# Row LSTM on one core: the odd pixels' output stays in PSUM for sum, difference and residual, the even residual moves to GpSimd, and the steady order is written anew

## The chip, the core and the metric

The kernel runs on one core of a Trainium2 chip. The engines are TensorE (PE in the profile; its weight loads are PEld), VectorE (DVE), ScalarE (ACT), GpSimd (POOL) and SyncE (SP, which here only issues DMAs). The metric is the device time of one execution in microseconds (us), as the median of several runs.

## The reference

The input x is 8 images of 96 channels, 128 x 128 pixels, in fp32. It is group-normalised, passed through a row LSTM and added to itself. The row LSTM goes down the rows of the image: each row's state depends on the row above, so the 128 rows cannot be computed at the same time.

```python
its = conv(X, W_is * mask, kernel 1x3) + b_is          # input part of the 4*96 gates
def step(carry, row_in):
    h, c = carry
    gates = conv(h, W_ss, kernel 3) + b_ss + row_in    # along the row
    f, i, o = sigmoid(...), sigmoid(...), sigmoid(...)
    g = tanh(...)
    c_new = f * c + i * g
    h_new = o * tanh(c_new)
    return (h_new, c_new), h_new
...
x = x + row_lstm(group_norm(x))
```

## The kernel before

**Half-steps.** The 8 images are split into two halves of 4, and the two run as two recurrences side by side. A half-step `n` is one row of one half; half-steps of the two halves alternate, and half 0 is one row ahead. So the result of half-step `n` is needed by half-step `n + 2`, and while it is being made the other half's products keep TensorE busy. There are 256 half-steps from 0 to 255 and one before; nearly all (2 to 253) run through one repeated order of work.

**Products.** Even and odd pixels of a row are kept apart, so that a product has 256 columns: 4 images by 64 pixel pairs. A half-step has three banks of gates, A, B and C, each one PSUM bank of 128 partitions by 512 columns, the left half for one and the right half for another partial product. The state enters the products in four forms: the sum of even and odd pixels ("vs", line 670), their difference ("vf", L674), and two shifted differences ("ve" in the tile te, L680, and "vo", L684). Products 1 and 2 take the sum and the difference; products 0 and 3 the shifted ones. P, Q and E are the products of the input rows ("xs"). Each product of one bank is two pieces, one for each row group of 64 partitions of the PE array, and the two row groups run at the same time. All are issued at line 512. After P, Q, 1 and 2, ScalarE copies the left half to SBUF (L583), VectorE adds the right half to it for the even pixels (L587) and subtracts it for the odd pixels (L591), and then 0, 3 and E are added on top.

**Gates.** ScalarE takes tanh (L596) and sigmoid (L615, and L618 for the last third of the output gate). VectorE multiplies the forget gate with the old cell state (L623); input gate times tanh is made by GpSimd for the even pixels (L630) and by VectorE for the odd ones (L632); then follow the new cell state (L642), its tanh on ScalarE into PSUM (L650) and the output h = o * tanh (L658), which is written into the tile hx. hx holds 128 partitions: 96 of the state, and 32 of normalised input channels which GpSimd (L337) and in part ScalarE (L335) write ahead. From hx come the sum, the difference and the shifted differences, and the residual (L700, VectorE, all 512 columns) adds h to the row of x that is stored.

**Input rows.** GpSimd also normalises the input (L337 into xw) and forms its sums and differences (L354, L358 into xs), one image and four rows at a time; this is the list of pieces that `work(n)` hands out, with the DMAs that go with them. `finish(n)` issues what is left of that list and the store of a finished block of four rows.

**Order.** The order on each engine is written by hand. The string PERIOD is one half-step's list, and each engine runs its own entries strictly in that order. An entry is a part's name and a bank; `a` and `b` at its end mean even and odd pixels; `'` means the half-step before, `+` the next one; for S, F, D0 and D1 (sum, difference, shifted even, shifted odd) two half-steps are added. `<` and `>` choose the row group. X and U are the pieces of `work` for hx on ScalarE and GpSimd; W1, W2, W3 are the three steps of the input rows. LAST is the list of the end. Names: cp copy, lo even (L587), hi odd (L591), ta tanh, si sigmoid, o2 the last third of the output gate, fg forget, gt gated, ce cell, th cell tanh, ou output, re residual.

**PSUM.** All gate banks come from one pool of 8 banks, three for a half-step, and are handed out in turn: a bank is written anew when everything that uses its earlier tile is through.

Of the kernel before, what the change touches and what calls it, by code (L numbers as in the profile page):

```python
# [8 lines left out]
AF = mybir.ActivationFunctionType  # L9
# [12 lines left out]
def kernel(  # L22
# [119 lines left out]
    hx = pair([P, R, 2, BH, JP], "hx")  # L142
# [274 lines left out]
    HB = BH * J  # L417
# [53 lines left out]
                self.waited = number  # L471

    lanes = Lanes()
    whole = slice(0, P)

    class HalfStep:


        def __init__(self, n):
            self.n, (self.row, self.s) = n, place(n)  # L480
            i, r = self.row // R % 2, self.row % R
            self.ps, self.m1, self.done, self.gates, self.outputs = {}, {}, set(), None, None
            self.moving = {"ve": te[self.s][:, i, r : r + 1]}
            self.started, self.images, self.halves, self.writer = set(), {}, {}, {}
            self.even_input = None
            self.hx, self.xs = hx[self.s][i][:, r], xs[self.s][i][:, r]
            self.c = cs[self.s].rearrange("p t b j -> p (t b j)")
# [164 lines left out]
        def output(self, lo=0, hi=BH, t=None):  # L652
            s, row = self.s, self.row
            nxt = hx[s][(row + 1) // R % 2][0:C, (row + 1) % R]
            self.h = strided(nxt[:, 0, 0, :], 0, [(BH * JP + 1, 2), (JP, BH), (1, J)])
            for t in range(2) if t is None else (t,):
                o, th = (self.part(ap, lo, hi, t) for ap in (self.o, self.tanh_of(t)))
                nc.vector.tensor_mul(self.h[:, t, lo:hi], o, th)  # L658

        def operand(self, name, parts=1):  # L660
            if name not in self.moving:
# [1 line left out]
            return self.moving[name].rearrange("p t (b j) -> p t b j", b=BH)  # L663

        def pair(self, lo, hi):
            return self.hx[:, 0, lo:hi, 0:J], self.hx[:, 1, lo:hi, 1 : J + 1]

        def total(self, engine=nc.vector, lo=0, hi=BH):
            e, o = self.pair(lo, hi)
# [20 lines left out]
        def residual(self, lo=0, hi=BH, t=None):  # L690
            s, row = self.s, self.row
            if t is not None:
                xo = xt[s, row // R][0:C, :, row % R, :].rearrange("p b (j t) -> p t b j", t=2)
                nc.vector.tensor_add(xo[:, t], xo[:, t], self.h[:, t])
                return
            xo = xt[s, row // R][0:C, :, row % R, :].rearrange("p b (j t) -> p t b j", t=2)
            if self.n < 1:
                nc.gpsimd.tensor_add(xo, xo, self.h)
            else:
                nc.vector.tensor_add(xo, xo, self.h)  # L700
# [31 lines left out]
    FIRST = [  # L732
        ([], own(0, 1, 1), own(0, 1, 2)),
        (shared(0, 1, 0), own(0, 1, 3), [(spare, 0, 1), (load_rows, 0, 2)]),
        (beside(0, 1, 1) + shared(0, 1, 2), own(1, 1, 0), []),
        (beside(0, 1, 3) + shared(1, 1, 0), own(1, 1, 1), []),
        (beside(1, 1, 1) + shared(1, 1, 2), own(1, 1, 2), []),
        (shared(1, 1, 3), own(1, 1, 3), [(spare, 1, 1), (load_rows, 1, 2), (load, 0, 2)]),
        (shared(0, 2, *SHARED[0]), own(0, 2, 0), []),
# [43 lines left out]
    def finish(n):  # L783
# [19 lines left out]
    LAST = (  # L803
        "2B'' 1A'' 1B'' 2A'' cpB'' 2C'' cpA'' loB'' hiB'' loA'' hiA'' 1C'' 0B'' EB'' 3A'' 0A'' "
        "3B'' cpC'' EA'' o2'' loC'' taA'' siA'' hiC'' 3C'' siBa'' 0C'' PA QA PB QB PC QC EA EB "
        "siBb'' fg'' taCb'' gtb'' taCa'' siC'' gta'' ceb'' thb'' cea'' oub'' tha'' oua'' F'' S'' "
        "D1'' D0'' re'' 1A 2A 1B 1C 2B 2C cpA loA hiA cpB loB 3A hiB 0A 0B 3B cpC loC hiC 0C 3C "
        "taA siA fg o2 siBa siBb taCa taCb gta gtb siC ceb cea thb tha oub oua reb rea"
    )
# [9 lines left out]
    }  # L819
    steps = {}  # L820

    def half_step(n):
        if n not in steps:
# [3 lines left out]
    def do(n, names, by_lanes=False):  # L827

        for name in names.split():
# [440 lines left out]
```

## Time and profile before

| | before |
|---|---|
| median of 3 runs | 2055.06 us (2054.9 to 2056.24) |
| the profiled execution | 2054.18 us, span 2052.4 us |
| granted TensorE clock | 0.995 |
| matmuls | 16400, one weight load each |
| DMA | 242.84 MB, mean 118 GB/s |

How to read the rows in the next sections. A row of totals gives the busy time of an engine, its share of the span and its instructions. A row of the stage table begins with the stretch (from:to in us from the span's start) and its length, then busy time and (xcount) for PE, PEld, DVE, ACT and POOL, then the granted clock, the DMA share and GB/s; for one line alone it has that line's engine only. A row of a timeline has the start in us, the duration in us (of all together where the count is over one), engine, line, operation, output and inputs, shape and count; in brackets the idle time before it and what ended it. A row of a group has line, engine, operation, tiles, shapes and count, then busy time in us and the mean in ns of one, then the idle time before it. A row of one source line gives the least, median and greatest duration in ns, and when it first and last ran.

### The profile page before, as it was taken

The page shows a single profiled execution, that of the slowest core. Times are in us where ns is not written, and L with a number is a line of the kernel's source. Part 1 is how long each engine was busy: PE and PEld are TensorE (multiplying, and loading weights), DVE is VectorE, ACT ScalarE, POOL GpSimd, SP SyncE. Part 2 cuts the span into 40 slices and gives each one's busy share as a digit, 9 for nine tenths or more (in the row PEclk, how much of TensorE's full clock was granted, in tenths as well). Part 3 has the DMA queues.
Part 4 walks back from the last instruction along what each step waited for, and adds up shares of the span by engine and source line. Part 5 has one row for each costly group of instructions (what it writes and reads, how often), then busy time and mean ns, then how long its engine had stood idle before and what let it go on. Part 6 is the DMA issues. An engine that isn't in the chain of part 4 may idle for free.

```text
span 2052.4 us, 46059 instructions
## 1 busy us (share of the span) xinstructions
PE 1980.4 (96%) x16400; PEld 1824.5 (89%) x16400; DVE 1904.3 (93%) x4018; ACT 1580.1 (77%) x3519; POOL 1568.0 (76%) x1917
## 2 busy tenths in 40 slices
PE   3679999999999999999999999999999999999998
PEld 0358999999999999999999999999999999999996
DVE  5788999999999999999999999999999999999997
ACT  6687777777777777777777777777777777777776
POOL 4358888888888888888888888888888888888851
PEclk9989999999999999999999999999999999999999
DMA  9983433444343344434334433433443343344311
GB/s 402 417 265 84 117 83 99 119 106 105 87 119 90 90 119 112 103 88 114 96 84 119 116 99 94 108 96 84 118 119 96 98 104 99 88 111 119 96 37 32
DMA packets 110290, 242.84 MB, mean 118 GB/s; under 512 B 6832, under 2 KB 16368, under 8 KB 104048
## 3 DMA queue, kind: packets, MB, share of 16 engines
q1 hardware_dynamic: 110064, 239.89, 43.0%
q8 instruction: 134, 2.20, 0.5%
q14 instruction: 92, 0.75, 0.1%
HBM read 181.34 MB, written 50.33 MB: 113 GB/s over the span
## 4 chain that ended last, share of the span: by engine, by line
PE 91%; DVE 3%; DMA 3%; ACT 2%; POOL 1%; issue 0%; SPq 0%; DVEq 0%; ACTq 0%; POOLq 0%
PE ps L512 90%; DMA xs<-in_x_dram 2%; DVE bst L1142 1%; DMA te<-in_x_dram 1%; DVE vf L674 0%; DVE ps L587 0%; ACT g L596 0%; DVE hx L658 0%; DVE vs L670 0%; POOL xw L337 0%; DVE ps L591 0%; DVE c L642 0%; ACT ps L615 0%; ACT ps L650 0%; PE rows L212 0%
## 5 line engine op out<-in xcount | busy, mean ns | idle before, releaser
L512 PE MATMUL ps<-vf,wm 64*128 64x256 f32 (+1 forms) x3046 | 847.2, 385 | 1.0 <-DVE vf L674 1.0
L512 PE MATMUL ps<-te,wl 64*128 64x256 f32 (+1 forms) x3042 | 790.1, 385 | 0.1
L512 PE MATMUL ps<-vo,wl 64*128 64x256 f32 (+1 forms) x3042 | 783.6, 382 | 2.2 <-DVE ps L591 2.1
L512 PE MATMUL ps<-vs,wm 64*128 64x256 f32 (+1 forms) x3046 | 748.0, 386 | 8.2 <-POOL vs L670 6.7
L512 PE MATMUL ps<-xs,wx 64*128 64x256 f32 (+1 forms) x3080 | 635.7, 377 | 2.0 <-POOL xs L354 1.8
L512 PEld LDWEIGHTS ps<-vf,wm 64*128 64x128 f32 (+1 forms) x3046 | 517.5, 186 | 22.6 <-DVE vf L674 2.9
L512 PEld LDWEIGHTS ps<-vs,wm 64*128 64x128 f32 (+1 forms) x3046 | 466.7, 186 | 41.7 <-POOL vs L670 9.5
L512 PEld LDWEIGHTS ps<-xs,wx 64*128 64x128 f32 x3080 | 490.9, 187 | 7.5 <-POOL xs L354 3.4
L512 PEld LDWEIGHTS ps<-vo,wl 64*128 64x128 f32 (+1 forms) x3042 | 458.2, 186 | 42.5 <-DVE ps L591 3.8
L512 PEld LDWEIGHTS ps<-te,wl 64*128 64x128 f32 (+1 forms) x3042 | 472.0, 186 | 20.9 <-PE ps L512 0.5
L583 ACT ACTIVATE m<-ps,wl 128x256 f32<-128x256 f32 x766 | 359.4, 469 | 95.1 <-PE ps L512 78.0
L630 POOL TENSOR_TENSOR g<-i,g 96x256 f32<-96x256 f32 x251 | 182.4, 727 | 307.8 <-ACT g L596 307.6
L587 DVE TENSOR_TENSOR ps<-m,ps 128x256 f32<-128x256 f32 x768 | 326.0, 425 | 17.8 <-ACT m L583 13.1
L591 DVE TENSOR_TENSOR ps<-m,ps 128x256 f32<-128x256 f32 x768 | 325.5, 424 | 17.5
L618 ACT ACTIVATE o<-ps 32x512 f32<-32x512 f32 x256 | 151.2, 591 | 224.2 <-PE ps L512 223.7
L596 ACT ACTIVATE g<-ps 32x512 f32<-32x512 f32 x765 | 313.6, 442 | 7.3 <-PE ps L512 0.6
L337 POOL TENSOR_SCALAR xw<-xr,rstd,nmr 128x512 f32<-128x512 f32 (+1 forms) x267 | 283.6, 1063 | 35.7 <-DVE nmr L329 11.5
L700 DVE TENSOR_TENSOR x<-x,hx 96x512 f32<-96x512 f32 x253 | 301.6, 1192 | 0.0
L512 PE MATMUL ps<-xs,wt 64*128 64x256 f32 x1012 | 299.2, 376 | 1.4 <-DVE ps L591 1.4
L358 POOL TENSOR_TENSOR xs<-xw 128x512 f32<-128x512 f32 (+1 forms) x254 | 293.0, 1154 | 0.0
L658 DVE TENSOR_TENSOR hx<-o,ps 96x256 f32<-96x256 f32 x512 | 213.4, 417 | 54.2 <-PE ps L512 30.5
L684 POOL TENSOR_TENSOR vo<-hx 128x256 f32<-128x256 f32 x257 | 258.7, 1006 | 5.7 <-PE ps L512 4.7
(118 smaller groups left out, 2569.3 us busy)
## 6 DMA issues: line engine op xcount, KB each, us to landing
xr<-in_x_dram SPq DMA_DIRECT2D x124, 512.0 KB, 6.4
x<-in_x_dram SPq DMA_DIRECT2D x62, 768.0 KB, 6.0
out_dram<-x SPq DMA_DIRECT2D x62, 768.0 KB, 4.8
xs<-in_x_dram SPq DMA_DIRECT2D x31, 1024.0 KB, 11.0
x<-in_x_dram SPq DMA_DIRECT2D x62, 256.0 KB, 3.1
te<-in_x_dram SPq DMA_DIRECT2D x8, 1024.0 KB, 11.2
hx<-in_x_dram SPq DMA_DIRECT2D x8, 1024.0 KB, 9.7
te<-xs SPq DMA_DIRECT2D x62, 128.0 KB, 3.2
```

The lines of the kernel that those rows point to most:

```text
L337: return engine.tensor_scalar(dst, src, scale, shift, ALU.mult, ALU.add)
L358: return engine.tensor_sub(differences, strided(xw[:, 0, :], 0, [(W + 1, n), (J + 1, 2), (1, J)]), strided(xw[:, 0, :], J, [(W + 1, n), (0 ...
L512: made = nc.tensor.matmul(self.ps[a][:, bass.ts(half, HB)][:, cols], weights[rows, bass.ts(a, P)], rhs[rows, cols], start=new, stop=False, ...
L583: nc.scalar.activation(self.m1[a], m1, AF.Identity, bias=column)
L587: nc.vector.tensor_add(self.ps[a][:, 0:HB], self.m1[a], self.ps[a][:, HB:])
L591: nc.vector.tensor_sub(hi, self.m1[a], hi)
L596: nc.scalar.activation(self.part(g, lo, hi, t), self.part(ps, lo, hi, t), AF.Tanh)
L618: nc.scalar.activation(self.o[C2:C], self.ps[1][C:P], AF.Sigmoid)
L630: nc.gpsimd.tensor_mul(to, i, g)
L658: nc.vector.tensor_mul(self.h[:, t, lo:hi], o, th)
L684: nc.gpsimd.tensor_sub(to, h[:, :, 0:J], h[:, :, 1 : J + 1])
L700: nc.vector.tensor_add(xo, xo, self.h)
```

## The change

The output of the odd pixels is no longer written to hx by VectorE. It is written over the cell tanh, in the right half of bank B of its half-step (`banked`, from half-step 2 on). Sum, difference and the odd half of the residual read it there. Two ScalarE copies are added: `keep_odd` ("co") copies it to hx, for the shifted difference D1, and `shared_odd` ("uo") copies the 32 normalised input channels of the next row's odd pixels from hx to the same place in PSUM, below the 96 rows of the state. The residual is split into even and odd pixels; the even half is a GpSimd instruction, the odd one stays on VectorE. PERIOD and LAST are written anew. In the first half-steps one normalisation (image 3 of half 0) moves from GpSimd in one half-step to ScalarE in the one before it. `finish` is called when both halves of the residual are done.

```diff
+            self.banked = self.n >= NH
...
-                nc.vector.tensor_mul(self.h[:, t, lo:hi], o, th)
+                to = th if t == 1 and self.banked else self.h[:, t, lo:hi]
+                nc.vector.tensor_mul(to, o, th)
+
+        @property
+        def odd_output(self):
+            return self.ps[1][:, HB:].rearrange("p (b j) -> p b j", b=BH)
+
+        def keep_odd(self):
+            if self.banked and self.row + 1 < NT:
+                nc.scalar.activation(self.h[:, 1], self.odd_output[0:C], AF.Identity)
+
+        def shared_odd(self):
+            if self.banked and self.row + 1 < NT:
+                i, r = (self.row + 1) // R % 2, (self.row + 1) % R
+                nc.scalar.activation(
+                    self.odd_output[C:P], hx[self.s][i][C:P, r, 1, :, 1 : J + 1], AF.Identity
+                )
...
         def pair(self, lo, hi):
-            return self.hx[:, 0, lo:hi, 0:J], self.hx[:, 1, lo:hi, 1 : J + 1]
+            before = steps.get(self.n - NH)
+            if before is not None and before.banked:
+                odd = before.odd_output[:, lo:hi]
+            else:
+                odd = self.hx[:, 1, lo:hi, 1 : J + 1]
+            return self.hx[:, 0, lo:hi, 0:J], odd
...
-                nc.vector.tensor_add(xo[:, t], xo[:, t], self.h[:, t])
+                h = self.odd_output[0:C] if t == 1 and self.banked else self.h[:, t]
+                engine = nc.gpsimd if t == 0 and self.n < last else nc.vector
+                engine.tensor_add(xo[:, t], xo[:, t], h)
...
-        (beside(0, 1, 1) + shared(0, 1, 2), own(1, 1, 0), []),
-        (beside(0, 1, 3) + shared(1, 1, 0), own(1, 1, 1), []),
+        (beside(0, 1, 1) + shared(0, 1, 2) + beside(0, 1, 3), own(1, 1, 0), []),
+        (shared(1, 1, 0), own(1, 1, 1), []),
...
     PERIOD = (
-        "1B> 1A< cpB 0C'> D0'' siBb' 2A< fg' 3C'> 2C< cpA taCb' loB hiB loA gtb' taCa' siC' gta' "
-        "QA+> hiA 1C< QB+> ceb' W3 QC< thb' PB+> 0B< 1C> EB< 2C> cea' oub' X U 3A< 0B> 0A< tha' "
-        "3B> oua' F' PC+< cpC 0A> PA+< 3A> 3B< EA> 2B+< S' 1A+> o2 loC taA 1B+< 2A+> W1+ siA hiC "
-        "3C< re' W2+ siBa D1' 2B+> 0C<"
+        "2B> 1C< taCb' hiA PA+> taCa' QB+< gtb' cpB QA+> gta' 0A< ceb' uo' 1C> loB 3A< siC' U "
+        "cea' 2C> EA< thb' hiB PC> tha' PB+< oub' X W1 QC+> EB< oua' cpC 0A> 0B< S' rea' 3A> loC "
+        "3B< F' W2 1B+> 1A+< taA hiC 0B> 2A+< D0' co' 3B> 3C< siA reb' W3 1A+> 0C< o2 fg 2A+> "
+        "1B+< siBa 0C> 2B+< cpA+ D1' 3C> 2C+< siBb loA+"
     )
...
-        "siBb'' fg'' taCb'' gtb'' taCa'' siC'' gta'' ceb'' thb'' cea'' oub'' tha'' oua'' F'' S'' "
-        "D1'' D0'' re'' 1A 2A 1B 1C 2B 2C cpA loA hiA cpB loB 3A hiB 0A 0B 3B cpC loC hiC 0C 3C "
+    "siBa'' siBb'' taCb'' taCa'' gtb'' gta'' ceb'' uo'' siC'' cea'' thb'' tha'' oub'' oua'' "
+    "rea'' co'' reb'' F'' S'' D1'' D0'' 1A 2A 1B 1C 2B 2C cpA loA hiA cpB loB 3A hiB 0A "
...
-        "re": "residual", "o2": "last_output_gate",
+        "re": "residual", "co": "keep_odd", "uo": "shared_odd", "o2": "last_output_gate",
...
-            if by_lanes and part == "re" and at < last:
+            if by_lanes and part == "re" and at < last and {"rea", "reb"} <= step.done:
                 finish(at)
```

More of the change, by code (lines that the diff above doesn't have):

```diff
@@ L473 @@
     lanes = Lanes()
+    steps = {}
     whole = slice(0, P)
@@ L797 @@
     PERIOD = (
-        "1B> 1A< cpB 0C'> D0'' siBb' 2A< fg' 3C'> 2C< cpA taCb' loB hiB loA gtb' taCa' siC' gta' "
-        "QA+> hiA 1C< QB+> ceb' W3 QC< thb' PB+> 0B< 1C> EB< 2C> cea' oub' X U 3A< 0B> 0A< tha' "
-        "3B> oua' F' PC+< cpC 0A> PA+< 3A> 3B< EA> 2B+< S' 1A+> o2 loC taA 1B+< 2A+> W1+ siA hiC "
-        "3C< re' W2+ siBa D1' 2B+> 0C<"
+        "2B> 1C< taCb' hiA PA+> taCa' QB+< gtb' cpB QA+> gta' 0A< ceb' uo' 1C> loB 3A< siC' U "
+        "cea' 2C> EA< thb' hiB PC> tha' PB+< oub' X W1 QC+> EB< oua' cpC 0A> 0B< S' rea' 3A> loC "
+        "3B< F' W2 1B+> 1A+< taA hiC 0B> 2A+< D0' co' 3B> 3C< siA reb' W3 1A+> 0C< o2 fg 2A+> "
+        "1B+< siBa 0C> 2B+< cpA+ D1' 3C> 2C+< siBb loA+"
     )
     LAST = (
-        "2B'' 1A'' 1B'' 2A'' cpB'' 2C'' cpA'' loB'' hiB'' loA'' hiA'' 1C'' 0B'' EB'' 3A'' 0A'' "
-        "3B'' cpC'' EA'' o2'' loC'' taA'' siA'' hiC'' 3C'' siBa'' 0C'' PA QA PB QB PC QC EA EB "
-        "siBb'' fg'' taCb'' gtb'' taCa'' siC'' gta'' ceb'' thb'' cea'' oub'' tha'' oua'' F'' S'' "
-        "D1'' D0'' re'' 1A 2A 1B 1C 2B 2C cpA loA hiA cpB loB 3A hiB 0A 0B 3B cpC loC hiC 0C 3C "
-        "taA siA fg o2 siBa siBb taCa taCb gta gtb siC ceb cea thb tha oub oua reb rea"
-    )
+    "1B'' 1A'' 2A'' 2B'' cpA'' 2C'' loA'' 1C'' hiA'' cpB'' 0A'' loB'' 3A'' EA'' hiB'' EB'' "
+    "cpC'' 0B'' loC'' 3B'' taA'' hiC'' 3C'' siA'' 0C'' PA QA PB QB PC QC EA EB o2'' fg'' "
+    "siBa'' siBb'' taCb'' taCa'' gtb'' gta'' ceb'' uo'' siC'' cea'' thb'' tha'' oub'' oua'' "
+    "rea'' co'' reb'' F'' S'' D1'' D0'' 1A 2A 1B 1C 2B 2C cpA loA hiA cpB loB 3A hiB 0A "
+    "0B 3B cpC loC hiC 0C 3C taA siA fg o2 siBa siBb taCa taCb gta gtb siC ceb cea thb tha "
+    "oub oua reb rea"
+  )
     PIXELS = {"a": (0, BH, 0), "b": (0, BH, 1)}
@@ L817 @@
         "S": "total", "F": "difference", "D0": "shifted_even", "D1": "shifted_odd",
[1 row of a table removed]
[1 row of a table added]
     }
-    steps = {}
     def half_step(n):
```

## The prediction

> **What bounds the kernel now.** First the page's totals, then the busy time by stage, then the timeline of one engine after another in a steady stretch.
>
> ```profile
> PE 1980.4 (96%) x16400; PEld 1824.5 (89%) x16400; DVE 1904.3 (93%) x4018; ACT 1580.1 (77%) x3519; POOL 1568.0 (76%) x1917
> 500.00:1000.00 500.00, 500.00 (x4296) 472.01 (x4295) 476.45 (x1007) 388.85 (x890) 406.96 (x470) 1.00 0.41 103
> 300.00:1900.00 1600.00, 147.04 (x215) 1.00 0.41 103
> ```
>
> The third row is the stage table for the forget product alone (L623), which runs once per half-step: 215 in 1600 us, so a half-step takes 7.442 us, and 500 us hold 67.2 of them. Dividing the second row by that: DVE is busy 7.09 us per half-step, ACT 5.79, POOL 6.06; ACT is idle 1.65. PE shows no gap, but its two row groups overlap, so its share hides stalls. Its floor comes from a dense stretch of one row group:
>
> ```profile
> 1011.66 0.38 PE L512 MATMUL ps<-vf,wm 64*128 64x256 f32 x1
> ...
> 1012.74 0.38 PE L512 MATMUL ps<-vs,wm 64*128 64x256 f32 x1
> ```
>
> These are the first and the last of six in that row group: five steps in 1.08 us, 0.216 each. A half-step has 4296 / 67.2 = 64 matmuls, 32 per row group: 6.90 us. A half (16 pieces of two matmuls, 0.431 a piece) is what a row group does. So 0.54 us per half-step is not matmul work. Where is it lost?
>
> ```profile
> 1007.25 0.89 DVE L658 TENSOR_TENSOR hx<-o,ps 96x256 f32<-96x256 f32 x2
> 1007.98 0.81 POOL L337 TENSOR_SCALAR hx<-x,rstd,nmr 32x512 f32<-32x512 f32 x1
> 1008.17 0.90 DVE L674 TENSOR_TENSOR vf<-hx 128x256 f32<-128x256 f32 x1
> 1008.99 0.41 DVE L670 TENSOR_TENSOR vs<-hx 128x256 f32<-128x256 f32 x1
> 1009.33 0.42 DVE L587 TENSOR_TENSOR ps<-m,ps 128x256 f32<-128x256 f32 x1
> 1010.12 1.25 DVE L700 TENSOR_TENSOR x<-x,hx 96x512 f32<-96x512 f32 x1
> 1010.77 1.06 POOL L684 TENSOR_TENSOR vo<-hx 128x256 f32<-128x256 f32 x1
> ...
> 1009.12 0.70 PE L512 MATMUL ps<-vf,wm 64*128 64x256 f32 x2
> 1009.46 0.79 PE L512 MATMUL ps<-vs,wm 64*128 64x256 f32 x4
> ```
>
> The difference (L674) and the sum (L670) have the same shape, yet one takes 0.90 and the other 0.41. The difference ends at 1009.07, 0.28 after GpSimd's instruction (1007.98 + 0.81 = 1008.79): it does not compute for 0.90, it is held until GpSimd is through. PE's products start 0.05 and 0.06 behind each result. Follow the loop from the sum at 1009.40 to the next one:
>
> ```profile
> 1011.49 0.47 ACT L583 ACTIVATE m<-ps,wl 128x256 f32<-128x256 f32 x1 [0.29 <-PE ps L512]
> 1011.86 0.37 ACT L615 ACTIVATE ps<-ps 96x256 f32<-96x256 f32 x1
> 1012.29 0.47 ACT L583 ACTIVATE m<-ps,wl 128x256 f32<-128x256 f32 x1
> 1012.79 0.65 ACT L596 ACTIVATE g<-ps 64x256 f32<-64x256 f32 x2
> 1013.52 0.72 POOL L630 TENSOR_TENSOR g<-i,g 96x256 f32<-96x256 f32 x1 [1.11 <-ACT g L596]
> 1014.21 1.15 POOL L358 TENSOR_TENSOR xs<-xw 128x512 f32<-128x512 f32 x1
> 1015.46 0.81 POOL L337 TENSOR_SCALAR hx<-x,rstd,nmr 32x512 f32<-32x512 f32 x1
> 1015.65 0.89 DVE L674 TENSOR_TENSOR vf<-hx 128x256 f32<-128x256 f32 x1
> 1016.47 0.41 DVE L670 TENSOR_TENSOR vs<-hx 128x256 f32<-128x256 f32 x1
> ...
> 1022.95 0.69 POOL L337 TENSOR_SCALAR hx<-x,rstd,nmr 32x384 f32<-32x384 f32 x1
> 1023.84 0.41 DVE L670 TENSOR_TENSOR vs<-hx 128x256 f32<-128x256 f32 x1
> ```
>
> Sum, PE's products, the copy of bank B (1011.49, waiting for PE), sigmoid, copy, two tanh, then GpSimd's three instructions without a gap, then the held difference, then the sum: 1016.47 - 1008.99 = 7.48 us. The check: where GpSimd's third instruction covers only 384 columns it is 0.12 shorter, and the next sum comes 1023.84 - 1016.47 = 7.37 later, 0.11 less. That is the loop.
>
> **The change, part by part.** *Sum, difference, residual of odd pixels.* What is held are the instructions with two SBUF inputs (L674, L700). Those with one PSUM input are not:
>
> ```profile
> L587 DVE TENSOR_TENSOR ps<-m,ps x768: 402/428/430, 86.3 to 2042.6; 128x256 f32<-128x256 f32 x192
> L632 DVE TENSOR_TENSOR g<-ps,g x256: 410/420/687, 119.9 to 2046.1; 96x256 f32<-96x256 f32 x127, 96x512 f32<-96x512 f32 x1
> L630 POOL TENSOR_TENSOR g<-i,g x251: 722/727/730, 168.8 to 2035.5; 96x256 f32<-96x256 f32 x126
> L698 POOL TENSOR_TENSOR x<-x,hx x2: 1291/1292/1293, 107.4 to 125.2; 96x512 f32<-96x512 f32 x2
> ```
>
> L587 spans 0.402 to 0.430 over 768 runs beside the same GpSimd work. With the odd half in PSUM no instruction of DVE's steady queue has two SBUF inputs, so I take 0.42 for sum, difference and odd residual each (bounds 0.41, as the free sum, and 0.90, held). DVE then has 6 x 0.43 + 0.42 (L632) + 4 x 0.42 + 3 x 0.42 + 0.69 for the forget product (147.04 / 215) = 6.63 at most, overlaps left in: off the bound. GpSimd no longer has to wait for DVE either:
>
> ```profile
> 160.41 0.80 POOL L337 TENSOR_SCALAR xw<-xr,rstd,nmr 128x512 f32<-128x512 f32 x1
> 181.34 0.61 POOL L684 TENSOR_TENSOR vo<-hx 128x256 f32<-128x256 f32 x1
> ```
>
> L684 takes 0.61 here against 1.06 beside L700, so some 0.45 of GpSimd's 6.06 was waiting.
>
> *Even residual on GpSimd.* In-place, stepped, two inputs: half of L698's 1.29 is 0.65, L630 (contiguous) 0.73; I take 0.8, bounds 0.65 to 1.29. GpSimd: 6.06 - 0.45 + 0.8 = 6.4, at most 7.35 with nothing freed and 1.29. Nothing critical waits for the residual itself, but the shifted differences (D0, D1) stand behind it in GpSimd's queue, and PE's first product with D1 is in the third slot of the next half-step. The store waits for both residuals; it has rows to spare.
>
> *Two copies on ScalarE.* keep_odd (96x256, PSUM to SBUF) and shared_odd (32x256 into PSUM) are new:
>
> ```profile
> L583 ACT ACTIVATE m<-ps,wl 128x256 f32<-128x256 f32 x201 | 94.4, 469 | 21.0 <-PE ps L512 16.4
> L650 ACT ACTIVATE ps<-c 96x256 f32<-96x256 f32 x135 | 51.8, 384 | 22.7 <-DVE c L642 17.8
> L615 ACT ACTIVATE o<-ps 64x512 f32<-64x512 f32 x67 | 39.6, 592 | 1.6
> L618 ACT ACTIVATE o<-ps 32x512 f32<-32x512 f32 x67 | 39.6, 591 | 59.9 <-PE ps L512 59.9
> L615 ACT ACTIVATE i<-ps 96x256 f32<-96x256 f32 x67 | 25.5, 381 | 1.6
> ...
> 1009.12 0.59 ACT L618 ACTIVATE o<-ps 32x512 f32<-32x512 f32 x1 [1.03 <-PE ps L512]
> 1009.62 0.57 ACT L596 ACTIVATE g<-ps 32x512 f32<-32x512 f32 x1
> 1010.22 0.57 ACT L615 ACTIVATE ps<-ps 96x512 f32<-96x512 f32 x1
> 1010.82 0.38 ACT L615 ACTIVATE i<-ps 96x256 f32<-96x256 f32 x1
> ```
>
> 256 columns without a bias cost 0.38 (L615, L650), so 2 x 0.38 = 0.76, bounds 0.37 and 0.47 each (the two 256-column groups' ends). ACT: 5.79 + 0.76 = 6.55 per half-step. It now sits on the path at every turn. In the new order its queue is taC (b, a), cpB, uo, siC, th (b, a), cpC, taA, co, siA, o2, siBa, cpA, siBb.
>
> *The new loop.* co reads the bank that S and F read on DVE, and stands behind F in the written order. No row shows two such readers of one bank; I take it that co waits for F, and bound it by not waiting. Times on ACT are from start to start. From F's end: a hop of 0.04 (PE's above were 0.05); co 0.38, siA 0.60 (1010.22 to 1010.82), o2 0.50 (1009.12 to 1009.62), siBa 0.38, cpA 0.37 (1011.49 to 1011.86), siBb 0.43 (1011.86 to 1012.29) = 2.66; two tanh 0.68, cpB 0.37, uo 0.38, siC 0.60, th 0.40, th 0.38 = 2.81; then DVE: hop 0.04, the last output product 0.42, hop 0.03, S 0.34 to loC's start (1008.99 to 1009.33), loC 0.42, F 0.42 = 1.67. Together 0.04 + 2.66 + 2.81 + 1.67 = **7.18 us**. If co does not wait, the path runs through PE: 3A's end, 0.21 to ACT (a matmul lasts 0.17 beyond its slot, hop 0.04), taA 0.57, the 2.66 and the 2.81, output and S with hops 0.95 = 7.20 to product 1B, and 16 pieces (6.90) until the next 3A of that chain: 14.10 for two half-steps, 7.05 each. PSUM: bank B now stays taken until the odd residual. F ends near PE's slot 11, 4.3 to 4.8 us into the half-step, the odd residual behind hiC 0.9 later; the next writer of the bank is slot 2 of the next half-step, 7.18 + 0.43 = 7.6, some 2 us later, so no stall.
>
> The Trainium skill, "PSUM — Partial Sum Buffer", section "PSUM bank collisions raise a hardware error", speaks against sharing this bank: two engines may not touch one bank in the same 32 partitions at once, reads against reads included. By it co must stand apart from F and the odd residual behind co, which gives the 7.18; without it the sum would be 7.05. No row of before shows such a pair.
>
> *Order, start and end.* FIRST moves one GpSimd piece to ACT in one half-step, LAST touches three half-steps; both count as nothing, within 2 us. GpSimd's own-row work comes a half-step later, which leaves two of the half-steps before its block's first product (a stall of PE's P products if that cover were gone). SP's DMAs are the same ones in the same order, issued behind the odd residual instead of the whole one.
>
> **Sum.** 250 steady half-steps (252 run the period, the first few are slower) x (7.442 - 7.18) = 65 us. Profiled time 2054.18 - 65 = 1989 us; the median shown, 2055.06, is 0.9 above it, which I leave aside.
>
> **Rivals.**
> *PE floor* (13%): hops and starts overlap better, as the pair of tanh does (0.65 for two), and co does not wait: 6.90 to 7.05, so 1918 to 1956. For: ACT's busy time 6.55 is under the floor. Against: PE then needs every operand in time.
> *GpSimd becomes the loop* (14%): stretched as today it needs 6.06 + 0.86 (the residual at two thirds of L698) + three gaps of 0.09 (as 1015.36 to 1015.46) = 7.19. It starts behind C's tanh, 0.21 + 0.65 + 0.08 into a half-step, so D1 reaches PE at 0.94 + 7.19 + 0.05 = 8.18; its slot opens at 7.18 + 0.86 = 8.04. The half-step becomes 7.32, 2024 us. Against: the stretching came from DVE's two-SBUF instructions.
> *ACT's waits stay* (9%): the slower side. Today ACT idles 1.65 us in waits for PE and DVE (0.89 of it at o2: 59.9 / 67). If the two copies only add to the queue, a half-step is 6.55 + 1.65 = 8.20, 190 us more, 2244. It decides at 7.44 - 6.55 = 0.89 us of waiting. Against: the new order puts siC and a copy where th waited, so I expect some 0.6 left, at taA.
> *The hold is not what two SBUF inputs do* (4%): F stays at 0.75, 0.33 more in the loop: 7.51, 2071 us.
> *No change* (5%): another loop near 7.44 that the present one covers.
>
> **How the numbers follow.** Forecast 55% (7.05 to 7.30, 1956 to 2018), floor 13%, GpSimd 14%, no change 5%, slower 13%. A measurement of this kernel can tell about 0.2%, 4 us. Faster 0.82, same 0.05, slower 0.13. The range 1925 to 2035 holds the forecast, nearly all of the GpSimd case and most of the floor, together 0.79.
>
> **What would show it.** Right: the forget product at about 223 per 1600 us; L674 and L670 both at 0.42 with no stretch; the even residual on GpSimd near 0.8; L684 near 0.61; ACT busy above 90%; ACT's copy waiting for DVE. Wrong: F still ending 0.28 behind a GpSimd instruction; PE waiting for vo (D1); ACT idle above 0.89 us per half-step.

## The result and the profile after

The changed kernel takes 2022.28 us (median of 4 runs, 2021.66 to 2023.0) against 2055.65 us of the kernel before on the same chip: the ratio is 0.9838, 95% interval 0.9821 to 0.9855. It is 33 us faster. The forecast was 66 us, so half of it came.

First the rows of the totals and of the stage table, which answer to the rows quoted before. The columns of the stage table are PE, PEld, DVE, ACT and POOL; the last row is the forget product alone.

```profile
PE 1946.5 (96%) x16400; PEld 1747.9 (87%) x16400; DVE 1617.9 (80%) x4018; ACT 1732.5 (86%) x4021; POOL 1560.3 (77%) x2169
500.00:1000.00 500.00, 500.00 (x4367) 458.83 (x4366) 405.49 (x1024) 436.29 (x1040) 408.99 (x545) 1.00 0.41 104
300.00:1900.00 1600.00, 152.32 (x219) 1.00 0.42 105
```

219 forget products in 1600 us make a half-step of 7.31 us; it was 7.44, and 250 times the difference is the 33 us. DVE fell from 7.09 to 5.93 us per half-step (405.49 / 68.4), ACT rose from 5.79 to 6.38. Neither is the bound. Now the groups of instructions between 500 and 1000 us, kept apart by form: busy time and mean ns, then the idle time before them and what ended it.

```profile
L693 DVE TENSOR_TENSOR vs<-hx,ps 128x256 f32<-128x256 f32 x68 | 28.6, 421 | 2.4
L719 DVE TENSOR_TENSOR x<-x,ps 96x256 f32<-96x256 f32 x68 | 28.4, 418 | 12.1 <-ACT hx L669 10.3
L697 DVE TENSOR_TENSOR vf<-ps,hx 128x256 f32<-128x256 f32 x68 | 28.4, 417 | 0.0
...
L674 ACT ACTIVATE ps<-hx 32x256 f32<-32x256 f32 x68 | 25.9, 381 | 1.7
L669 ACT ACTIVATE hx<-ps 96x256 f32<-96x256 f32 x68 | 25.9, 381 | 3.8 <-DVE vf L697 1.5
...
L719 POOL TENSOR_TENSOR x<-x,hx 96x256 f32<-96x256 f32 x68 | 50.3, 740 | 6.9 <-DVE hx L661 3.2
...
L707 POOL TENSOR_TENSOR vo<-hx 128x256 f32<-128x256 f32 x68 | 41.8, 615 | 0.0
```

Every duration of the forecast is there: sum 0.421, difference 0.417, odd residual 0.418, the two copies 0.381 each, the even residual 0.740 on GpSimd, and vo at 0.615 (it was 1.06). The hold is gone. What is not there is the forecast's loop: the copy that keeps the odd output (L669, "co") waited for the difference 1.5 us in the whole stretch.

The loop that does set the time is one half-step of the timeline (start, duration, engine and line, and in brackets the idle time before). It starts with the sum and ends with the next one. For PE only the rows of the row group marked `>` are shown; the first of them holds a piece of each group. PEld is PE's weight load.

```profile
1009.45 0.42 DVE L693 TENSOR_TENSOR vs<-hx,ps 128x256 f32<-128x256 f32 x1
...
1009.92 0.30 PEld L514 LDWEIGHTS ps<-vs,wm 64*128 64x128 f32 x4 [0.28 <-DVE vs L693]
1009.92 0.70 PE L514 MATMUL ps<-vs,wm 64*128 64x256 f32 x4
...
1010.11 0.42 DVE L697 TENSOR_TENSOR vf<-ps,hx 128x256 f32<-128x256 f32 x1
...
1010.46 0.38 PE L514 MATMUL ps<-vo,wl 64*128 64x256 f32 x1
...
1010.89 0.38 PE L514 MATMUL ps<-te,wl 64*128 64x256 f32 x1
...
1011.34 0.48 PE L514 MATMUL ps<-vs,wm 64*128 64x256 f32 x1
...
1011.66 0.38 PE L514 MATMUL ps<-vs,wm 64*128 64x256 f32 x1
...
1011.88 0.38 PE L514 MATMUL ps<-vf,wm 64*128 64x256 f32 x1
...
1012.31 0.44 PE L514 MATMUL ps<-vo,wl 64*128 64x256 f32 x1
...
1012.80 0.38 PE L514 MATMUL ps<-te,wl 64*128 64x256 f32 x1
...
1013.43 0.65 ACT L598 ACTIVATE g<-ps 64x256 f32<-64x256 f32 x2 [0.18 <-PE ps L514]
...
1014.61 0.38 ACT L674 ACTIVATE ps<-hx 32x256 f32<-32x256 f32 x1
...
1015.53 0.69 ACT L652 ACTIVATE ps<-c 96x256 f32<-96x256 f32 x2
...
1016.28 0.41 DVE L661 TENSOR_TENSOR hx<-o,ps 96x256 f32<-96x256 f32 x1
1016.73 0.42 DVE L693 TENSOR_TENSOR vs<-hx,ps 128x256 f32<-128x256 f32 x1
```

From the sum's end at 1009.87 to C's tanh at 1013.43 are 3.56 us: seven pieces of PE in their written order. From there to the end of the pair of cell tanh (1016.22) are 2.79, with the copy of the shared odd rows (L674, "uo") among them, and the output product and the sum take 0.93 more, to 1017.15. Together 7.28 us, the distance of the two sums. Two waits show the loop from both ends: PE's weight load waits for the sum (0.28), and C's tanh for PE (0.18).

The seven pieces would take 7 x 0.431 from 1009.92 if they followed each other densely, and C's tanh could start 0.20 later (a matmul lasts 0.17 beyond its slot, and then comes the hop from PE to ScalarE) at 1013.14. It starts 0.29 later. The gaps say where: 0.54 from the first piece to the second, then 0.43, 0.45, 0.54, 0.43, 0.49. In the piece that begins at 1011.34 the second matmul follows 0.32 after the first, not 0.216. The code makes a piece wait where the other row group wrote the same bank last, and the other group is itself late: its products with the difference cannot begin before that ends, at 1010.53. What removes these 0.29 is tested below: neither an early sum nor an early difference does so alone.

### The profile page after: what moved, and what is told of

The parts are those of the page before. It is cut to its first block, busy times and chain, and to the rows that moved or that the text cites. A ratio compares the mean times of both kernels' runs of the same rounds, so it can differ in the third digit from the quotient of the medians.

```text
span 2020.2 us, 47123 instructions
## 1 busy us (share of the span) xinstructions
PE 1946.5 (96%) x16400; PEld 1747.9 (87%) x16400; DVE 1617.9 (80%) x4018; ACT 1732.5 (86%) x4021; POOL 1560.3 (77%) x2169
## 4 chain that ended last, share of the span: by engine, by line
PE 92%; DMA 3%; ACT 2%; DVE 2%; POOL 1%; issue 0%; SPq 0%; DVEq 0%; POOLq 0%; ACTq 0%
PE ps L514 92%; DMA xs<-in_x_dram 2%; DVE bst L1167 1%; DMA te<-in_x_dram 1%; ACT g L598 0%; POOL xw L337 0%; ACT m L585 0%; ACT ps L617 0%; PE rows L212 0%; ACT o L620 0%; PE pv L291 0%; ACT hx L335 0%; ACT xr L223 0%; ACT ps L652 0%; ACT o L617 0%
## 5 line engine op out<-in xcount | busy, mean ns | idle before, releaser
L514 PE MATMUL ps<-vs,wm 64*128 64x256 f32 (+1 forms) x3046 | 795.4, 402 | 8.4 <-POOL vs L693 5.7
L514 PE MATMUL ps<-te,wl 64*128 64x256 f32 (+1 forms) x3042 | 689.9, 377 | 0.0
L514 PE MATMUL ps<-xs,wx 64*128 64x256 f32 (+1 forms) x3080 | 528.2, 377 | 2.1 <-POOL xs L354 1.9
L514 PEld LDWEIGHTS ps<-vs,wm 64*128 64x128 f32 (+1 forms) x3046 | 420.4, 186 | 88.6 <-DVE vs L693 71.3
L514 PEld LDWEIGHTS ps<-xs,wx 64*128 64x128 f32 x3080 | 413.0, 187 | 7.9 <-POOL xs L354 3.4
L617 ACT ACTIVATE ps<-ps 96x512 f32<-96x512 f32 (+1 forms) x512 | 244.4, 477 | 0.4
L337 POOL TENSOR_SCALAR xw<-xr,rstd,nmr 128x512 f32<-128x512 f32 (+1 forms) x267 | 210.4, 789 | 35.6 <-DVE nmr L329 11.5
L644 DVE TENSOR_TENSOR c<-ps,g 96x256 f32<-96x256 f32 (+1 forms) x507 | 211.7, 418 | 8.9 <-POOL g L632 0.3
L719 POOL TENSOR_TENSOR x<-x,hx 96x256 f32<-96x256 f32 x252 | 186.5, 740 | 40.8 <-DVE hx L661 27.8
L337 POOL TENSOR_SCALAR hx<-x,rstd,nmr 32x512 f32<-32x512 f32 (+1 forms) x245 | 191.5, 781 | 24.7
```

Source lines behind the costliest of these rows:

```text
L337: return engine.tensor_scalar(dst, src, scale, shift, ALU.mult, ALU.add)
L514: made = nc.tensor.matmul(self.ps[a][:, bass.ts(half, HB)][:, cols], weights[rows, bass.ts(a, P)], rhs[rows, cols], start=new, stop=False, ...
L617: nc.scalar.activation(to, gate, AF.Sigmoid)
L644: nc.vector.tensor_add(c, f, g)
L719: engine.tensor_add(xo[:, t], xo[:, t], h)
```

## The experiments

"Half-step" below is 7.31 us plus the difference of the medians from 2022.28 us, divided by 250; the counts of forget products agree with it to 0.05. Ratios are against the kernel before, measured beside each run at 2052.2 to 2055.7 us, so that medians of different experiments can be up to 3 us apart for that alone.

### The parts of the change, one by one

**The data path alone, in the old order.** PERIOD of before, with the copies put in; FIRST, LAST and all else as in the changed kernel:

```diff
- "... taCa' siC' gta' ... hiC 3C< re' W2+ ..."
+ "... taCa' siC' uo' gta' ... hiC 3C< rea' co' reb' W2+ ..."
```

> The new data path (output in PSUM, two ScalarE copies, even residual on GpSimd) in the order of before. If the data path carries the gain, the difference (L674 of before) is no longer held by GpSimd, which is worth 0.47 us of the 7.44 in a half-step, and the copies give back some 0.2: 7.2, 1990 to 2005 us. If the gain needs the new order, the copies cost what the hold gave: 2040 to 2070 us.

Measured: 2070.9 us, ratio 1.0091 (1.0061 to 1.012), slower than before: near the second figure expected, but not for its reason. The waits between 500 and 1000 us (total, times, longest) say why:

```profile
DVE x L719 <- ACT hx L669: 91.0, 67, 1.5
```

The odd residual waits 1.36 us in each half-step for co, which reads the same bank and which ScalarE reaches late, behind bank A's sigmoid. VectorE stands still for it. So the same kernel once more with the copy behind the odd residual:

```diff
- "... rea' co' reb' ..."
+ "... rea' reb' co' ..."
```

> As the run with the new data path in the order of before, but keep_odd stands behind the odd residual in the written order, so that VectorE does not wait for ScalarE there (91 us of such waits in 500 us in that run). If this wait is what made that run slower than before: 0.3 to 0.5 less per half-step, 1950 to 2000 us. If the two copies in the old ScalarE queue are: 2050 to 2070 us.

Measured: 2018.3 us, ratio 0.9828 (0.9799 to 0.9856). One place in the order is worth 53 us, and the data path with the old order is as good as the whole change. The gain is less than expected (1950 to 2000), as with the change itself. Why two so different orders come out equal was not looked into.

**The new order without the output in PSUM.** `banked` is false: the odd output goes to hx, there are no copies, and sum, difference and odd residual have two SBUF inputs as before. The even residual stays on GpSimd.

```diff
-            self.banked = self.n >= NH
+            self.banked = False
```

> The new order and the even residual on GpSimd, but the odd output goes to hx as before and no copy is made. Theory (the loop runs from the sum through PE's pieces up to 3C, the tanh of C, ScalarE's queue, the output and back to the sum, 7.28 us): the copy uo leaves that loop (0.38 less) and the hold on sum and difference comes back (some 0.3 to 0.5 more): 2015 to 2055 us. Rival (the new order alone makes the gain): 2022 or below, with sum and difference at 0.42.

Measured: 2120.61 us, ratio 1.0333 (1.0303 to 1.0363), slower than either theory had it. The hold now strikes another instruction:

```profile
1006.35 0.91 POOL L354 TENSOR_TENSOR xs<-xw 128x256 f32<-128x256 f32 x1
...
1006.92 2.30 DVE L719 TENSOR_TENSOR x<-x,hx 96x256 f32<-96x256 f32 x1
...
1007.22 0.61 POOL L703 TENSOR_TENSOR te<-hx 96x256 f32<-96x256 f32 x1
...
1007.79 1.16 POOL L358 TENSOR_TENSOR xs<-xw 128x512 f32<-128x512 f32 x1
```

The odd residual, 0.42 when free, is held for 2.30 us, past the end of two GpSimd instructions, until 0.27 behind the third (7.79 + 1.16 = 8.95; it ends at 9.22). The kernel before had 0.28 there. Of the 254 odd residuals the median takes 2.30 and the longest 3.42. The Trainium skill ("SBUF — State Buffer", "Who interferes with whom") says that a VectorE instruction with two SBUF inputs and a GpSimd instruction that reads SBUF exclude each other for a whole instruction; the trace agrees that one is held, and shows that the one that waits can miss several turns. So the order needs the data path; the data path does not need the order.

**The even residual back on VectorE**, behind the odd one:

```diff
-                engine = nc.gpsimd if t == 0 and self.n < last else nc.vector
+                engine = nc.vector
...
- "... S' rea' 3A> ... siA reb' W3 ..."
+ "... S' 3A> ... siA reb' rea' W3 ..."
```

> The even residual goes back to VectorE, behind the odd residual; GpSimd is without it, everything else as in the changed kernel. It is then the only instruction of VectorE in a half-step with two SBUF inputs. Theory (such an instruction is held until a row of GpSimd's instructions without a gap has ended, and the forget product, which ScalarE's queue and the cell wait for, stands behind it): the even residual takes over 1 us, the half-step grows by 0.1 to 0.5, 2045 to 2150 us. Rival (VectorE has some 0.8 us of waiting per half-step for bank A's copy, and GpSimd loses 0.74 of work): the hold is covered, 2005 to 2030 us.

Measured: 2023.29 us, ratio 0.9857 (0.9843 to 0.9872): no difference from the change. A miss; the rival was right. The instruction is held, to 0.85 in the row below (median 0.76, longest 2.10), and VectorE's wait for bank A's copy, 54.2 us in this stretch of the changed kernel, takes it up:

```profile
DVE ps L589 <- ACT m L585: 14.3, 56, 0.4
...
1005.79 0.85 DVE L719 TENSOR_TENSOR x<-x,hx 96x256 f32<-96x256 f32 x1
```

Moving the even residual to GpSimd is worth nothing in this order.

### Which loop

**Without co.** From half-step 16 on the odd output is not copied to hx.

```diff
-            if self.banked and self.row + 1 < NT:
+            if self.banked and self.row + 1 < NT and self.n < 2 * NH * R:
```

> Leaves keep_odd out from half-step 16 on, so D1 reads old values. Theory (the loop through PE and the tanh of C, in which keep_odd does not stand, and ScalarE waits 0.18 for PE before that tanh): no more than 5 us faster, 2017 to 2024, and the wait before the tanh of C grows to some 0.5. Rival, the prediction's loop (the difference, keep_odd, five ScalarE instructions, tanh of C and on): 0.38 less in the loop, 1930 to 1980 us.

Measured: 2021.46 us, ratio 0.985 (0.9821 to 0.9878). Leaving co out changes nothing. The loop of the forecast, which goes from the difference through co, does not bind.

**Without uo.** The same condition in `shared_odd`.

> Leaves shared_odd out from half-step 16 on, so the 32 input channels of odd pixels in sum and difference are whatever the bank holds. Theory (shared_odd stands in the loop): the sum 0.3 earlier, and ScalarE's queue gives the next bound, 0.18 less: 1975 to 1995 us. Rival (PE's exposed weight loads): 2015 to 2022 us. Rival (the whole loop follows): 0.38 less, 1925 to 1940 us.

Measured: 1971.39 us, ratio 0.9599 (0.9571 to 0.9627), half-step 7.11, just below the range of the theory. The 0.38 us of this copy is worth 0.20 per half-step, and PE's wait for the sum, 18.6 us in the changed kernel, is gone:

```profile
PEld ps L514 <- DVE vs L693: 1.3, 8, 0.2
...
1002.29 0.71 PE L514 MATMUL ps<-vs,wm 64*128 64x256 f32 x4
...
1005.79 0.65 ACT L598 ACTIVATE g<-ps 64x256 f32<-64x256 f32 x2 [0.18 <-PE ps L514]
```

So uo stands in the loop that binds, as the timeline above has it, and another limit follows at 7.11. But the seven pieces are no faster: from the first of them to C's tanh are 3.50 us here, 3.51 in the changed kernel, although PE does not wait for the sum.

**Without both copies.**

> Both copies are left out from half-step 16 on (the odd output is then not kept in SBUF, and the shared odd rows not brought into the bank), everything else as in the changed kernel. Theory A (the loop of bank A's tanh, with the kept copy in it, is the one at 7.09): without that copy it loses 0.38, the half-step falls to 6.92 to 7.02, 1930 to 1955 us. Theory B (TensorE's pieces with their own stalls are 7.09): as with the one copy left out, 1963 to 1975 us.

Measured: 1943.66 us, ratio 0.9463 (0.9447 to 0.9479), half-step 7.00, as theory A had it. Once uo is gone, co counts. Here PE's rows from the first piece after the sum to C's tanh are

```profile
1006.44 0.64 PE L514 MATMUL ps<-vs,wm 64*128 64x256 f32 x4
...
1009.71 0.65 ACT L598 ACTIVATE g<-ps 64x256 f32<-64x256 f32 x2 [0.16 <-PE ps L514]
```

3.27 us, against 3.51 in the changed kernel and 3.22 dense. Here the two row groups run in step, and nearly all of the stalls go. So they are not a fixed cost of the seven pieces. A sum in time is not enough for that, as the run before shows; here the difference is earlier too, and ends 0.38 behind the start of the first piece instead of 0.61.

**The difference ahead of bank C's add** on VectorE, so that PE does not wait for it:

```diff
- "... 3A> loC 3B< F' W2 ..."
+ "... 3A> F' 3B< loC W2 ..."
```

> The changed kernel with F ahead of loC on VectorE and nothing else. F ends 0.33 earlier, the sum as before, hiC some 0.1 later. Theory (the late difference costs PE's pieces between the sum and 3C some 0.1): 2000 to 2015 us. Rival (the pieces lose their time at the waits between the two row groups, not at F): 2018 to 2026 us.

Measured: 2018.05 us, ratio 0.9826 (0.9798 to 0.9855), at most 4 us better than the change and inside its interval, and just in the rival's range. The difference now ends 0.28 behind the start of the first piece, and yet from that piece to C's tanh are 3.54 us (1006.99 to 1010.53). An early difference alone does not remove the stalls either.

### Where else can the copy stand?

**uo behind both cell tanh**, ahead of bank C's copy:

```diff
- "... ceb' uo' 1C> ... tha' PB+< oub' X ..."
+ "... ceb' 1C> ... tha' PB+< oub' uo' X ..."
```

> shared_odd moved on ScalarE's queue from ahead of the output gate to behind both cell tanh. Theory (loop through ScalarE's queue between the tanh of C and the cell tanh): the sum ends 0.23 to 0.31 earlier in the half-step, of which 0.1 to 0.25 is kept, the difference being as late as it was: 1960 to 2000 us. Rival (PE's own pieces with their exposed weight loads set 7.28 whatever the sum does): 2018 to 2026 us.

Measured: 2038.69 us, ratio 0.9935 (0.9913 to 0.9958): slower than the change, and outside both ranges. The copy waits for the output product, which uses the same bank; C's copy and then C's add wait behind it, and the difference, behind the add, comes late for PE:

```profile
PEld ps L514 <- DVE vf L697: 10.9, 18, 0.6
```

With the difference ahead of the add, as above:

> As the run with shared_odd behind the cell tanh, and the difference F ahead of loC on VectorE, so that it no longer stands behind the copy of C. In that run the sum was not late, the difference was (1010.46, behind loC at 1010.12). Theory (loop from the sum and the difference through PE to the tanh of C): F ends some 0.45 earlier than there, PE's product 2A does not wait, 1975 to 2010 us. Rival (PE's exposed weight loads alone): 2018 to 2026 us. Rival (ScalarE's queue is full, so any move on it costs): 2035 or more.

Measured: **2009.3 us** (2008.0 to 2010.6), ratio 0.9784 (0.9755 to 0.9812). This is the fastest kernel with both copies in it, 11 us below the change by the ratios, and its interval lies under that of the change. The copy runs beside the output product, though it still waits for a part of it, and the sum for the copy:

```profile
ACT ps L674 <- DVE ps L661: 17.4, 69, 0.3
...
DVE vs L693 <- ACT ps L674: 6.3, 34, 0.2
```

**uo a turn earlier, behind the last output gate.** This takes it out of the loop shown above altogether.

```diff
- "... ceb' uo' 1C> ... 0C< o2 fg ..."
+ "... ceb' 1C> ... 0C< o2 uo fg ..."
```

> The copy of the shared odd rows (0.38 us on ScalarE) is moved from behind C's tanh and B's copy to behind the last output gate, a turn earlier, everything else as in the changed kernel. Theory (the half-step of 7.28 is one loop: sum, seven pieces of TensorE's row group up to bank C, C's tanh, 2.79 us of ScalarE with this copy in it, output product, sum; leaving the copy out altogether gave 51 us): ScalarE's part of the loop becomes 2.41, TensorE's wait for the sum (18.6 us in 68 times, 0.27 each) goes, and tanh of C is late by 0.38 less its slack of 0.18; the half-step falls to 7.05 to 7.15, 1975 to 1995 us. Rival (ScalarE's own queue is the bound, and the copy costs 0.38 wherever it stands): 2015 to 2040.

Measured: 2079.02 us, ratio 1.0128 (1.0113 to 1.0143), half-step 7.54. A clear miss. PE no longer waits for the sum (0.2 us in the stretch), but another loop has taken over:

```profile
1007.03 0.59 ACT L598 ACTIVATE g<-ps 32x512 f32<-32x512 f32 x1 [0.84 <-PE ps L514]
...
1009.18 0.38 ACT L674 ACTIVATE ps<-hx 32x256 f32<-32x256 f32 x1
...
1010.00 0.47 ACT L585 ACTIVATE m<-ps,wl 128x256 f32<-128x256 f32 x1
...
1010.97 0.43 DVE L593 TENSOR_TENSOR ps<-m,ps 128x256 f32<-128x256 f32 x1
...
1011.55 0.45 PE L514 MATMUL ps<-vo,wl 64*128 64x256 f32 x1
```

Tanh of bank A (1007.03), ScalarE's queue with uo in it, bank A's copy (1010.00), its two adds on VectorE (the second ends at 1011.40), then bank A's next product (1011.55); that bank's products lead to the next tanh of A. Call this the loop of bank A. From tanh to copy are 2.97, so the rest of it is 7.54 - 2.97 = 4.57. The changed kernel has 2.41 there (1010.09 to 1012.50). If its rest is the same, its loop of bank A takes 6.98, hidden 0.33 behind the sum's loop.

With the difference first as well:

> As the run before, and the difference stands ahead of the add to bank C on VectorE. Theory: the difference is in time for TensorE's second piece of the other row group as it was when the order alone was changed (4 us there): 1970 to 1995 us, at most 5 below the run before. Rival: with the sum no longer waited for, the lateness of the difference is hidden, or bank C's add becomes late: no gain, or up to 10 us more than the run before.

Measured: 2077.6 us, ratio 1.0121 (1.0104 to 1.0138): no gain, as the rival had it.

**uo behind bank A's copy**, out of that loop too:

```diff
- "... 2B+< cpA+ D1' 3C> ..."
+ "... 2B+< cpA+ uo D1' 3C> ..."
```

> The copy of the shared odd rows stands behind the copy of bank A and ahead of the sigmoid before C's tanh; everything else as in the changed kernel. Theory (two loops: from the sum through TensorE and C's tanh back to the sum, with this copy in it 7.28; from bank A's tanh through ScalarE's queue to bank A's copy, its adds and products, with this copy in it 7.55, without it 7.1): the copy stands in neither, the half-step is 7.09 to 7.17, 1970 to 1995 us. Rival (C's tanh is late by 0.38 less its slack of 0.18, and the rest of the queue with it; ScalarE's sum sets the time): 2010 to 2030 us.

Measured: 2041.84 us, ratio 0.9936 (0.9919 to 0.9953), half-step 7.39. Again a miss, and again a loop:

```profile
1003.54 0.59 ACT L598 ACTIVATE g<-ps 32x512 f32<-32x512 f32 x1 [0.84 <-PE ps L514]
...
1007.23 0.65 ACT L598 ACTIVATE g<-ps 64x256 f32<-64x256 f32 x2
...
1009.10 0.42 DVE L593 TENSOR_TENSOR ps<-m,ps 128x256 f32<-128x256 f32 x1
...
1009.57 0.48 PE L514 MATMUL ps<-xs,wt 64*128 64x256 f32 x1
...
1010.89 0.59 ACT L598 ACTIVATE g<-ps 32x512 f32<-32x512 f32 x1 [0.84 <-PE ps L514]
```

Tanh of A, now without a gap on ScalarE to C's tanh 3.69 later; C's tanh releases VectorE's gates, and behind these stands bank B's second add, which ends at 1009.52; PE's next product of bank B starts 0.05 later, and A's next tanh follows. The rest of this loop is 7.39 - 3.69 = 3.70; the changed kernel has 3.34 from A's tanh to C's, which with the same rest makes 7.04.

With the difference first, and then with co behind bank A's copy as well:

> As the run before, with the difference ahead of bank C's add on VectorE. Theory: the half-step is that of the loop of bank A, where TensorE's second product of bank A waits for the difference; 0 to 8 us less than the run before, 1965 to 1990. Rival: no difference between the two (within 3 us).

Measured: 2029.9 us, ratio 0.9886 (0.9865 to 0.9906), 12 us less than the run before, more than its theory had, but slower than the change.

```diff
- "... D0' co' 3B> ... 2B+< cpA+ uo D1' ..."
+ "... D0' 3B> ... 2B+< cpA+ co' uo D1' ..."
```

> As the run before, and the copy that keeps the odd output moves behind bank A's copy too, out of the loop of bank A; the odd residual on VectorE no longer waits for it but it for the residual. Theory (the loop of bank A is the one behind): that loop loses 0.38, and the half-step falls to TensorE's 6.90 with its stalls or to C's tanh, late behind both copies: 7.0 to 7.1, 1955 to 1980 us. Rival (the queue of ScalarE between bank A's tanh and C's tanh, which both copies lengthen wherever they stand in it, sets the time): equal to the run before within 5 us.

Measured: 2096.12 us, ratio 1.02 (1.0184 to 1.0215), half-step 7.61. Both of its theories failed. From A's tanh to C's are now 3.95:

```profile
1006.59 0.59 ACT L598 ACTIVATE g<-ps 32x512 f32<-32x512 f32 x1 [0.84 <-PE ps L514]
...
1010.54 0.66 ACT L598 ACTIVATE g<-ps 64x256 f32<-64x256 f32 x2
```

With the 3.70 of the run above this gives 7.65, and 7.61 was measured: the loop over C's tanh and bank B, longer than before, since ScalarE also waits for PE within it.

**The copies on VectorE.** uo on VectorE, where it idles for bank A's copy:

```diff
-                nc.scalar.activation(
-                    self.odd_output[C:P], hx[self.s][i][C:P, r, 1, :, 1 : J + 1], AF.Identity
-                )
+                nc.vector.tensor_copy(
+                    self.odd_output[C:P], hx[self.s][i][C:P, r, 1, :, 1 : J + 1]
+                )
...
- "... ceb' uo' 1C> ... 0C< o2 fg ..."
+ "... ceb' 1C> ... 0C< o2 fg uo ..."
```

> VectorE copies the shared odd rows, behind the forget product, where it idles 0.71 us for bank A's copy; ScalarE is without that copy, everything else as in the changed kernel. Theory (the 0.38 on ScalarE stands in one of several nearly equal loops wherever it is put): it is out of all of them, the half-step is that of the kernel without the copy, 7.09, 1965 to 1985 us. Rival (the copy has an SBUF input and is held by GpSimd, or ScalarE's sigmoid of bank B's even half waits for it, since the two touch one bank): 2000 to 2040 us.

With the difference first as well:

> As the run before, with the difference ahead of bank C's add. Theory (the next loop passes through bank A's products, the second of which waits for the difference): 3 to 12 us less than the run before, 1955 to 1980. Rival: within 3 us of it.

And with `keep_odd` as a VectorE copy too:

```diff
- "... D0' co' 3B> 3C< siA reb' W3 ..."
+ "... D0' 3B> 3C< siA reb' co' W3 ..."
```

> As the run before, and VectorE does the copy that keeps the odd output too, behind the odd residual. Theory: ScalarE is at 5.63 us per half-step and no loop holds a copy on it; the half-step goes to TensorE's floor of 6.90 with its stalls, 6.97 to 7.06, 1935 to 1965 us. Rival (the forget product, now behind two more instructions of VectorE, and bank A's adds behind it become late): equal to the run before or slower by up to 30 us.

Measured: 2077.89 us (ratio 1.0115, 1.0099 to 1.0132), 2077.2 us (1.0115, 1.0099 to 1.013) and 2058.97 us (1.0026, 1.0017 to 1.0035), half-steps 7.53, 7.53 and 7.46: the first lies outside both ranges, the second bears out its rival, and the third is faster than the second, but far from its theory. The copy itself takes 0.43 and is not held, but in the first of the three

```profile
ACT i L617 <- DVE ps L674: 39.6, 66, 0.9
...
1005.68 0.59 ACT L598 ACTIVATE g<-ps 32x512 f32<-32x512 f32 x1 [0.90 <-PE ps L514]
...
1008.38 0.38 ACT L617 ACTIVATE i<-ps 96x256 f32<-96x256 f32 x1 [0.61 <-DVE ps L674]
1008.66 0.46 ACT L585 ACTIVATE m<-ps,wl 128x256 f32<-128x256 f32 x1
```

ScalarE's sigmoid of bank B waits 0.61 for the copy, since both touch bank B. It reads partitions 0 to 95, the copy writes 96 to 127. The Trainium skill ("PSUM — Partial Sum Buffer", "PSUM bank collisions raise a hardware error") lets two engines use one bank at once in different groups of 32 partitions; no run here shows them at once, because this program orders the two by the bank. The loop of bank A explains the times: tanh to copy is 2.98 here, 2.98 + 4.57 = 7.55 for the measured 7.53. In the third kernel it was 2.91 (1005.11 to 1008.02), 7.48 for 7.46. The first rival named this wait, but priced it too low.

## Where the prediction was right and where it failed

- **What bound the kernel before, and what the data path removes: right.** The held difference was the loop's last step; with one input in PSUM the three instructions take 0.42, as forecast, and GpSimd's vo 0.615. The data path carries the whole gain (2018.3 us in the old order, with co in the right place); the new order without it is slower than before.
- **The even residual on GpSimd: right in size (0.740 for 0.8), wrong in use.** Nothing critical waited for it, but nothing was won by it either.
- **The two copies: right in size (0.381 for 0.38).** C's tanh to the end of the cell tanh took 2.79 for the forecast's 2.81, and from there to the sum 0.93. This stretch of the loop was right.
- **"The new loop" is the step that failed.** The prediction closed the loop from the difference over co and ScalarE's queue to C's tanh, 7.18 us. Co waits for the difference hardly ever (1.5 us in 500), because ScalarE reaches it late, after waiting for PE ahead of A's tanh (0.76 us in the timeline), and without co the time is the same. The loop that binds goes from the sum over PE to C's tanh. The prediction considered PE only as 16 dense pieces over two half-steps (7.05) and left out that seven pieces stand in the written order between the sum and C's tanh, in one half-step. Dense, these give 0.05 + 3.22 + 2.79 + 0.93 = 6.99, under the 7.18; with the 0.29 of stalls 7.28. So the term that was mis-sized is PE's: 0.431 a piece was taken from a dense stretch, and the seven pieces behind a late sum took 3.51 - 0.20 = 3.31, which is 0.47 each. With that, the loop that the forecast had left out became longer than the one it had chosen.
- **The shared bank.** The forecast's rule that the readers of one bank follow one another was right for this program, but the price lay elsewhere: not co waiting for the difference, but the odd residual waiting for co (0.15 per half-step after the change, 1.36 in the old order with co ahead of it), and in other orders ScalarE waiting for uo.
- **The rivals and the signs.** The range of 1925 to 2035 holds the result, but by the room that it left for the rivals: the forecast loop itself had 1956 to 2018. ScalarE's idle time fell from 1.65 to 7.31 - 6.38 = 0.93 us per half-step, not to the 0.6 expected; over 0.89 was named as a sign of being wrong, and it came. ScalarE was busy for 86%, not above 90%. That GpSimd's rival had 2024 us, close to the 2022.28 measured, is luck: GpSimd is busy for 5.98 us per half-step (408.99 / 68.4) and idles 70.8 us in the stretch waiting for C's tanh. PE did not reach its floor. Without both copies the half-step is 7.00, in the floor's range of 6.90 to 7.05: the copies are what keeps the kernel from it.
- **What stays open.** What makes the seven pieces 0.29 longer than dense. A row group's wait for the other in the same bank was not taken away by itself; an early sum alone and an early difference alone leave the stretch at 3.50 and 3.54, and only without both copies is it 3.27. That either late operand is enough would fit these three; but in the kernel of 2009.3 us both are in time (the sum ends at 1002.95 and the difference at 1003.29, for a first piece at 1003.16), and the last two of its six gaps are still 0.53 and 0.51. Also open is why the half-step stops at 7.11 without uo: by the two relations above the loop of bank A would be 2.39 + 4.57 = 6.96 there (A's tanh at 1002.49, bank A's copy at 1004.88) and the one over C's tanh 3.30 + 3.70 = 7.00, and yet co is worth 0.11.

## What to carry to other kernels

Where several engines are busy for more than 80% of a half-step, find the second and the third loop before forecasting: freeing one step of 0.3 us can win only the distance to the next loop. Walk each loop through TensorE's queue in its written order, and allow for stalls there, not only dense matmuls: here the pieces took 0.47 us each, for 0.431 dense. Before adding an instruction to a shared queue or a shared PSUM bank, write down every loop that passes through its place; here a copy of 0.38 us cost 0.15 to 0.43 us per half-step, against the kernel without it, wherever it was put, and least where it ran beside the output product that the loop waits for anyway and the difference came first (2009.3 us).

## What the runs showed of the hardware

A VectorE instruction with two SBUF inputs, 0.42 us when free, was held beside GpSimd instructions without a gap: in the new order without the output in PSUM for 2.30 us at the median and 3.42 at most, in the row shown past the ends of two GpSimd instructions. The difference of the kernel before, which ended 0.28 behind the first GpSimd instruction, had shown only the mild form. With one input in PSUM, sum, difference and odd residual took 0.417 to 0.421 beside the same work. GpSimd was stretched too: its residual took 0.98 at the median in that new order and 0.74 in the changed kernel, where no VectorE instruction of the steady order has two SBUF inputs.
